# Second linear layer of a graph network: seven products in fourteen batches instead of ten, sums of h made in place, and a new order of VectorE's work

## The chip, the cores and the metric

The kernel runs on one core of one Trainium2 chip. The metric is the device time of one execution in microseconds. Before the change it is 2470.86 us, the median of three runs (2469.76 to 2471.12).

## What is computed

The input x has 16 batches of 1024 rows and 256 channels. A first layer (graph weights, attention with four heads, residual, layer norm) gives x1. The second layer, which the change touches, is

```
agg = A_hat @ x1                        # per batch
h   = relu(batchnorm(agg @ W1.T + b1))  # 512 features, statistics over all batches
o   = h @ W2.T + b2                     # 256 features
out = layernorm(x1 + batchnorm(o))      # statistics of o over all batches
```

All is in float32. Both batch norms need statistics over all 16 batches, so each is a barrier: h is written to HBM as it is made and read back once its statistics are complete, and o is held in SBUF for all batches until its own are complete.

## The kernel before, in words

Matrices are kept transposed, features on the 128 partitions and the 1024 rows of a batch along the free dimension. h of one batch is four blocks of 128 x 1024, one for each 128 of its 512 features. It is loaded as two tiles ("parts"): part i holds blocks i and i + 2. W2 gives two output blocks of 128 x 1024 per batch.

The stage of the second linear layer is the loop over 16 batches at L1798. For each batch ScalarE applies scale, shift and relu of the first batch norm to the four blocks of the next batch's h in place (`scale_shift1`, L1674), PE multiplies, and the result is moved out of PSUM into `o2T[b]` with the bias added; VectorE takes the statistics of four pieces of 128 x 512.

There are two ways to multiply. The undivided one (batches 0 and 11 to 15) uses 16 matmuls of 128 x 512 per batch at L1846 and moves each output block out with one VectorE pass of 128 x 1024 at L1873, followed by two statistics at L1877. The other (batches in `SEVEN`, 1 to 10) treats the product as a 2 x 2 block product and needs seven block products of two matmuls each at L1772: 14 matmuls. It needs four sums of quarters of W2, made once by GpSimd (`left_sums`, into the tile `w2S`), and four sums of quarters of h per batch, made by VectorE (`h_sums`, L1741 to L1752), each on two halves (i = 0 and 1), which is eight instructions of 128 x 512. The sums go into the output tiles of the last four batches, which are not yet in use: batches 12 to 15, two tiles for even and two for odd batches. That is why `SEVEN` ends where it does.

`products` (L637) puts the seven products in the order p1, p6, p2, p7, p5, p4, p3 over three PSUM banks per batch, a, b and c. p1 is copied by ScalarE (L656) into a temporary; p2 is added by PE onto p1 in bank a and moved out by ScalarE (L669). p6 goes into bank b and VectorE adds p1's copy (L648); p7 is added by PE onto p6 in the same bank, which has to wait until VectorE has read it, and VectorE adds p1 again; p4 is added onto that, and VectorE makes an output piece of it. p5 goes into bank c and p3 onto it, each followed by a VectorE add (L679, L687). So VectorE has five passes out of PSUM per batch. The three temporaries lie in the next batch's output tile.

The order of work on PE, ScalarE and VectorE is the order in which the code calls it (`manual_schedule`). [...] The order of the loads on SP is decided by the scheduler. Tiles of h have four buffers, two batches: a load of the next batch's part starts when the batch before the present one has been read for the last time, which is p3's first matmul for part 0 and its second for part 1.

In a seven-product batch b the calls for VectorE were, in order: the third and fourth sums of half 1; a statistic of the batch before; p6's add; two such statistics; p7's add; the statistic (b, 0); p5's add; the first and second sums of the next batch, half 0; p4's add; the same for half 1; p3's add; the third and fourth sums of the next batch, half 0. For batch 1 the sums were made after batch 0's outputs had been moved out and their statistics taken.

After the loop, `coefficients2` gives the second batch norm's scale and shift, and a tail over 16 batches scales o, transposes it on PE, adds x1 (loaded into tiles `xf` by `load_x1`) and applies the layer norm. The x1 of batches 0, 1 and 2 go into three tiles: two held h of batch 0, the third holds `w2S`.

Of the kernel before, what the change touches and what calls it, by code (L numbers as in the profile page):

```python
# [13 lines left out]
ALU = mybir.AluOpType  # L14
# [5 lines left out]
HALF = 512  # L20
# [495 lines left out]
def fast_path(  # L516
# [19 lines left out]
    nc = tc.nc  # L536
    B, N, C = x.shape
# [158 lines left out]

    def right_sums(eng, T, b11, b12, b21, b22):

# [5 lines left out]
    H0, H1 = slice(0, HALF), slice(HALF, N)  # L704
    C0, C1 = slice(0, P), slice(P, C)
# [18 lines left out]
    xp = ctx.enter_context(tc.tile_pool(name="xp", bufs=3))  # L724
# [10 lines left out]
    with (  # L735
# [449 lines left out]
        def run(fs, k):  # L1185
            for f, a in fs[:k]:
                f(*a)
            del fs[:k]
# [135 lines left out]
        with tc.manual_schedule(  # L1324
# [64 lines left out]
            for j in range(len(bursts)):  # L1389
                b, u = j // PERB, j % PERB  # L1390
# [75 lines left out]
            j = len(bursts)  # L1466
# [24 lines left out]
    w1T, w2T = wl["w1T"], wl["w2T"]  # L1491
# [26 lines left out]
    with (  # L1518
# [123 lines left out]
        for b in range(1, B):  # L1642
# [3 lines left out]
            elif b == B - 1:  # L1646
                h0 = []
                for i in range(2):
                    t = xp.tile([P, 2, N], F32, tag="x", name=f"hl_0_{i}")
# [3 lines left out]
            for i, step in enumerate(steps):  # L1653
                step()
                if i == len(steps) - 1 and b < B - 1:
                    later = linear1(b)
# [22 lines left out]
        t = agg.pop(B - 1)  # L1679
# [28 lines left out]
    with tc.tile_pool(name="hl", bufs=4) as hl, tc.tile_pool(name="o2p", bufs=1) as o2p:  # L1708
        o2T = [
            o2p.tile([P, CC, N], F32, tag=f"o2_{b}", name=f"o2_{b}") for b in range(B)  # L1710
        ]
# [3 lines left out]
        def load_x1(b, pool, tag):  # L1715
            xf[b] = pool.tile([P, NCH, C], F32, tag=tag, name=f"xf_{b}")
            nc.sync.dma_start(xf[b], x1_d[b])
# [5 lines left out]
        parts = {}  # L1723

        def load_h(b):
            parts[b] = [hl.tile([P, 2, N], F32, tag="hl", name=f"hl_{b}_{i}") for i in range(2)]
            for i in range(2):
                nc.sync.dma_start(parts[b][i], h_d[b][:, i::2, :])
            hs_of[b] = [parts[b][k % 2][:, k // 2, :] for k in range(HC)]

        SEVEN = range(1, B - 5)
        w2S = xp.tile([P, 4, 2, P], F32, tag="x", name="w2S")
        K0, K1 = slice(0, HC // 2), slice(HC // 2, HC)
        left_sums(
# [1 line left out]
            w2T[:, K0, C0], w2T[:, K1, C0], w2T[:, K0, C1], w2T[:, K1, C1],  # L1738
        )

        def h_sums(b, i, later):  # L1741

            t = parts[b][i]
            T = [o2T[B - 4 + 2 * (b % 2) + j // 2][:, i, (j % 2) * HALF : (j % 2 + 1) * HALF]
                 for j in range(4)]
            b11, b12, b21, b22 = t[:, 0, H0], t[:, 0, H1], t[:, 1, H0], t[:, 1, H1]
            if not later:
                nc.vector.tensor_tensor(T[0], b12, b11, ALU.subtract)
                nc.vector.tensor_tensor(T[1], b22, T[0], ALU.subtract)
            else:  # L1750
                nc.vector.tensor_tensor(T[2], b22, b12, ALU.subtract)
                nc.vector.tensor_tensor(T[3], b21, T[1], ALU.subtract)  # L1752

        def linear2_seven(b):
            X = parts[b]
            hs_of.pop(b)

            def T(j, i):
                return o2T[B - 4 + 2 * (b % 2) + j // 2][:, i, (j % 2) * HALF : (j % 2 + 1) * HALF]

            def mm(k, ps, start):
                for i in range(2):
                    left, right = {
                        1: (w2T[:, i, C0], X[i][:, 0, H0]),
                        2: (w2T[:, 2 + i, C0], X[i][:, 1, H0]),
                        3: (w2S[:, 3, i, :], X[i][:, 1, H1]),
                        4: (w2T[:, 2 + i, C1], T(3, i)),
                        5: (w2S[:, 0, i, :], T(0, i)),
                        6: (w2S[:, 1, i, :], T(1, i)),
                        7: (w2S[:, 2, i, :], T(2, i)),  # L1770
                    }[k]
                    nc.tensor.matmul(  # L1772
                        ps, left, right, start=(start and i == 0), stop=(i == 1),
                        skip_group_check=True,
                    )

            def bank(name):
                if name[0] == "c":
                    return tile_s(name)[:, H0]
                return {"a": tile_o, "b": tile_t}[name[0]](name)  # L1780

            def temps(key, name):
                k = ("p1", "u2", "u3").index(key)
                return o2T[b + 1][:, k // 2, (k % 2) * HALF : (k % 2 + 1) * HALF]

            out = [o2T[b][:, c, hs] for c in range(CC) for hs in (H0, H1)]
            bias = (cols["b2"][:, 0:1], cols["b2"][:, 1:2])
            return products(f"o{b}", bank, out, mm, temps, bias)

        def statistics2(b, i):  # L1790
            c, half = i // 2, i % 2
            nc.vector.bn_stats(
                bn2_st[:, c, 2 * b + half, :], o2T[b][:, c, half * HALF : (half + 1) * HALF]
            )

        load_h(1)
        rest = []
        for b in range(B):  # L1798
            if b + 2 < B and b not in SEVEN:
                load_h(b + 2)  # L1800
            if b in SEVEN:
                nxt = b + 1
                if b > 1:
                    load_h(nxt)
                p1, p6, p2, p7, p5, p4, p3 = linear2_seven(b)
                p1()
                h_sums(b, 1, True)
                run(rest, 1)
                p6()
                run(rest, 1)  # L1810
                p2()
                run(rest, 1)
                for k in (0, 2):
                    scale_shift1(hs_of[nxt][k], k)
                p7()
                statistics2(b, 0)
                p5()
                for k in (1, 3):
                    scale_shift1(hs_of[nxt][k], k)
                if nxt in SEVEN:  # L1820
                    h_sums(nxt, 0, False)
                p4()
                if nxt in SEVEN:
                    h_sums(nxt, 1, False)
                p3()
                if nxt in SEVEN:
                    h_sums(nxt, 0, True)
                rest = [(statistics2, (b, i)) for i in (3, 2, 1)]
                if nxt not in SEVEN:
                    run(rest, 3)  # L1830
                    load_h(nxt + 1)
                continue
            if b + 1 < B:
                for k in (0, 2, 1, 3):
                    scale_shift1(hs_of[b + 1][k], k)
            h = hs_of.pop(b)
            pss = [tile_s(f"po2_{b}_{c}") for c in range(CC if b < B - 1 else CC - 1)]
            last_ps = [tile_o(f"po2_last_{half}") for half in range(2 if b == B - 1 else 0)]

            def half_ps(c, hs):  # L1840
                if last_ps and c == CC - 1:
                    return last_ps[0 if hs == H0 else 1]
                return pss[c][:, hs]

            def mm(c, k, hs):
                nc.tensor.matmul(  # L1846
                    half_ps(c, hs), w2T[:, k, c * P : (c + 1) * P], h[k][:, hs],
                    start=(k == 0), stop=(k == HC - 1),
                )

            if b == 0:

                for ks in (range(HC // 2), range(HC // 2, HC)):
                    for c in range(CC):
                        for k in ks:
                            for hs in (H0, H1):
                                mm(c, k, hs)
            for c in range(CC):
                last = b == B - 1 and c == CC - 1
                if b:  # L1860
                    for k, hs in (
                        [(k, hs) for hs in (H0, H1) for k in range(HC)] if last
                        else [(k, hs) for k in range(HC) for hs in (H0, H1)]
                    ):
                        mm(c, k, hs)
                if last:
                    for hs in (H0, H1):
                        nc.scalar.activation(
                            o2T[b][:, c, hs], half_ps(c, hs), AF.Identity,
                            bias=cols["b2"][:, c : c + 1],  # L1870
                        )
                else:
                    nc.vector.tensor_scalar(  # L1873
                        o2T[b][:, c, :], pss[c], cols["b2"][:, c : c + 1], None, ALU.add
                    )
                for half, hs in enumerate((H0, H1)):
                    nc.vector.bn_stats(bn2_st[:, c, 2 * b + half, :], o2T[b][:, c, hs])  # L1877
                if b == B - 1:
                    coefficients2(c)
            if b == 0:  # L1880
                for i, later in ((0, False), (1, False), (0, True)):
                    h_sums(1, i, later)
            if b >= B - 3:
                load_x1(b - (B - 3), xp, "x")

# [171 lines left out]
```

## Time and profile before

| what | value |
|---|---|
| median of 3 runs | 2470.86 us |
| the profiled execution, time | 2469.28 us |
| its span (first to last instruction) | 2467.5 us |
| PE busy | 2425.2 us, 98% of the span |
| DVE (VectorE) busy | 1840.3 us, 75% |
| ACT (ScalarE) busy | 1231.6 us, 50% |
| POOL (GpSimd) busy | 479.9 us, 19% |
| mean granted TensorE clock | 0.998 |
| stage of the second linear layer, first matmul to the tail's first | 2165.22 to 2373.19 us |
| an f32 matmul of 128 x 512 (L1772) | two records, 592 ns each, started 0.43 us apart |
| a sum of 128 x 512 on VectorE (L1748 to L1752) | 675 to 693 ns |

Times in a trace count from the start of the span. The name a_o stands for bank a of any batch, since buffer numbers are left out, and o for the output tile o2T of any batch, po for the PSUM tile of the undivided way. A line such as L648 is a line of the code above; a line in a helper serves several callers. An arrow <- in square brackets names what ended the idle time before an instruction. PEld is PE's weight load, which carries the waits of the matmul that it precedes. A busy engine isn't a bound by itself: what counts is which engine's work the chain of waits runs through in the stage concerned.

### The profile page before, as it was taken

To read this page: it belongs to the slowest core of one execution; us is meant where nothing else is said; L and a number is where in the kernel's file an instruction comes from. 1 tells how busy PE (TensorE), PEld (TensorE's weight loads), DVE (VectorE), ACT (ScalarE), POOL (GpSimd) and SP (SyncE) were. 2 spreads that over 40 slices of the span, in tenths; PEclk is the share of its full clock that TensorE was granted. 3 is DMA by queue.
4 is the path that set the end of the run, shared out by engine and by line. 5 is a ranking of instruction groups with operands and counts; after the bars stand their busy time and mean duration, and the time that the engine had idled before them with its cause. 6 is when DMAs were issued, how large, how long until landed. Compare 5 with 4: busy or idle time off the path is not lost.

```text
span 2467.5 us, 32796 instructions
## 1 busy us (share of the span) xinstructions
PE 2425.2 (98%) x12462; PEld 1035.2 (42%) x12462; DVE 1840.3 (75%) x2528; ACT 1231.6 (50%) x1535; POOL 479.9 (19%) x487
## 2 busy tenths in 40 slices
PE   8999999999999999999999999999999999999997
PEld 4343443443434434434434343344444444434455
DVE  5678878878888888788788888856555555578568
ACT  6375665765765766757657667311010010144458
POOL 0021112211211211121112113522112212000026
PEclk9999999999999999999999999999999999999999
DMA  3123232332232231323322327222122122255559
GB/s 136 31 48 84 54 53 69 69 51 67 39 82 60 41 86 54 52 69 69 53 68 47 72 52 116 54 101 102 69 86 102 68 85 102 91 200 175 182 190 340
DMA packets 414647, 220.42 MB, mean 89 GB/s; under 512 B 353168, under 2 KB 386448, under 8 KB 406032
## 3 DMA queue, kind: packets, MB, share of 16 engines
q1 hardware_dynamic: 409120, 167.36, 27.6%
q0 software_dynamic: 4832, 50.34, 4.9%
q8 instruction: 100, 1.64, 0.3%
q14 instruction: 67, 0.55, 0.1%
q10 hardware_dynamic: 528, 0.52, 0.1%
HBM read 134.49 MB, written 83.69 MB: 88 GB/s over the span
## 4 chain that ended last, share of the span: by engine, by line
PE 83%; DVE 10%; ACT 3%; DMA 2%; issue 1%; SPq 0%; POOL 0%; DVEq 0%; POOLq 0%
PE ps L1066 17%; PE po L1087 17%; PE pgb L896 7%; PE b_agg L1564 4%; PE pga L896 4%; PE c_agg L1564 4%; PE pk L993 3%; PE po L1846 3%; PE pv L1006 2%; PE a_agg L1564 2%; PE b_h L1596 2%; PE b_o L1772 2%; PE pgc L896 2%; PE pgd L896 2%; PE c_h L1596 2%; PE c_o L1772 1%
## 5 line engine op out<-in xcount | busy, mean ns | idle before, releaser
L1071 ACT ACTIVATE p<-ps 128x1024 f32<-128x1024 f32 x512 | 497.4, 1021 | 182.2 <-PE ps L1066 123.2
L1097 DVE TENSOR_TENSOR acc<-acc,p 128x1024 f32<-128x1024 f32 x384 | 501.4, 1306 | 52.3 <-ACT p L1071 28.9
L1066 PE MATMUL ps<-qT,kT 64*64 64x512 f32 x4096 | 488.3, 592 | 0.3 <-ACT p L1071 0.3
L1087 PE MATMUL po<-p,v 64*64 64x512 f32 x4096 | 485.6, 589 | 0.0
L1161 POOL TENSOR_TENSOR o<-o,r_all 128x512 f32<-128x512 f32 x62 | 95.9, 1555 | 1104.8 <-DVE r_all L1155 989.9
L1087 PEld LDWEIGHTS po<-p,v 64*64 64x64 f32 x4096 | 159.4, 133 | 280.1 <-issue 273.2
L1066 PEld LDWEIGHTS ps<-qT,kT 64*64 64x64 f32 x4096 | 152.4, 133 | 285.9 <-issue 248.5
L847 DVE SCALAR_TENSOR_TENSOR wg<-wg,adj_s 128x1024 f32<-128x1024 f32 x128 | 149.7, 1217 | 24.6 <-ACT wg L843 24.6
L838 ACT ACTIVATE wg<-crow,ccol 128x1024 f32<-128x1024 f32 x128 | 146.7, 1146 | 6.1 <-PE pg L978 6.1
L843 ACT ACTIVATE wg<-wg 128x1024 f32<-128x1024 f32 x128 | 135.9, 1062 | 0.9
L993 PE MATMUL pk<-xT,kvw_s 128*128 128x512 f32 x256 | 121.9, 598 | 3.1 <-ACT drow L1140 3.1
L1006 PE MATMUL pv<-kvw_s,xT 128*128 128x256 f32 x512 | 123.9, 385 | 0.0
L1006 PEld LDWEIGHTS pv<-kvw_s,xT 128*128 128x128 f32 x512 | 95.0, 190 | 50.3 <-issue 13.6
L906 ACT ACTIVATE qT<-qT 128x512 f32<-128x512 f32 x60 | 37.1, 626 | 149.8 <-DVE qT L909 145.3
L896 PE MATMUL pgb<-wg,S 128*128 128x512 f32 x240 | 111.0, 605 | 0.0
L896 PE MATMUL pga<-wg,x 128*128 128x512 f32 x240 | 109.6, 599 | 0.7 <-ACT qT L919 0.7
L1564 PE MATMUL a_agg<-ahT,x1l 128*128 128x512 f32 x240 | 108.1, 593 | 0.7 <-ACT agg L1312 0.7
L1564 PE MATMUL b_agg<-aT,x1S 128*128 128x512 f32 x240 | 107.9, 592 | 0.0
L1162 POOL TENSOR_TENSOR x<-x,o 128x512 f32<-128x512 f32 x62 | 106.9, 1734 | 2.4
L656 ACT COPY p_agg<-a_agg 128x512 f32<-128x512 f32 x15 | 8.8, 586 | 183.3 <-PE a_agg L1564 179.5
L1675 ACT ACTIVATE hl<-hl,bn_sh,bn_sg 128x1024 f32<-128x1024 f32 x64 | 75.6, 1232 | 40.7 <-DMA hl<-h 38.1
L692 POOL TENSOR_TENSOR x1S<-x1l 128x512 f32<-128x512 f32 x15 | 19.4, 1293 | 352.9 <-PE c_agg L1564 350.1
(234 smaller groups left out, 3495.8 us busy)
## 6 DMA issues: line engine op xcount, KB each, us to landing
h<-hw POOLq DMA_DIRECT2D x16, 2048.0 KB, 6.6
hl<-h SPq DMA_DIRECT2D x32, 1024.0 KB
x<-x POOLq DMA_DIRECT2D x16, 1024.0 KB, 4.3
x1l<-x SPq DMA_DIRECT2D x16, 1024.0 KB
xf<-x SPq DMA_DIRECT2D x16, 1024.0 KB
o<-oS SPq DMA_DIRECT2D x62, 256.0 KB
o<-o SPq DMA_DIRECT2D x248, 64.0 KB
x<-in_x_dram SPq DMA_DIRECT2D x15, 1024.0 KB
```

The costliest lines, as they stand in the source:

```text
L838: nc.scalar.activation(w, s["crow"], AF.Abs, bias=s["ccol"][:, n : n + 1])
L843: nc.scalar.activation(w, w, AF.Tanh, scale=0.5)
L847: nc.vector.scalar_tensor_tensor(w, w, 1.0, adj_s[:, n, :], op0=ALU.subtract, op1=ALU.mult)
L896: nc.tensor.matmul(ps, left, right, start=(start and i == 0), stop=(i == NCH // 2 - 1), skip_group_check=True,)
L993: nc.tensor.matmul(ps, kvw_s[:, c, kc * P : (kc + 1) * P], s["xT"][:, c, hs], start=(c == 0), stop=(c == CC - 1),)
L1006: nc.tensor.matmul(pt[:, j * C : (j + 1) * C], s["xT"][:, c, n * P : (n + 1) * P], kvw_s[:, c, C : 2 * C], start=(c == 0), stop=(c == CC - 1),
L1066: nc.tensor.matmul(ps[kh * D : (kh + 1) * D, hd * HALF : (hd + 1) * HALF], kT[r, pr, ks], qT[r, pr, qh * HALF : (qh + 1) * HALF], start=Tr ...
L1071: nc.scalar.activation(p, ps, AF.Exp)
L1087: nc.tensor.matmul(g["po"][kh][hd * D : (hd + 1) * D, :], s["v"][r, m, h * D : (h + 1) * D], p[r, hd * HALF : (hd + 1) * HALF], start=(m = ...
L1097: nc.vector.tensor_add(g["acc"], g["acc"], p)
L1162: nc.gpsimd.tensor_tensor(xs, xs, o, ALU.add)
L1564: nc.tensor.matmul(ps, left, right, start=(start and i == 0), stop=(i == NCH // 2 - 1), skip_group_check=True,)
```

## The change

`SEVEN` grows from batches 1 to 10 to batches 1 to 14. The sums of h no longer need four spare output tiles: three of the four overwrite a quarter of h that no later product needs, and one goes into a quarter of the last batch's output tile (`second_sum`; even and odd batches have a half each). Since a sum overwrites h, the third sum now waits until p1 has read its quarter, and the fourth until p2 has. The temporaries of `products` go into the batch's own output pieces. The calls are reordered, so that VectorE has mostly one statistic or one sum between two of its passes out of PSUM, where there were up to four. The first two sums of batch 1 are called ahead of batch 0's moves out of PSUM. The calls of `load_x1` for batches 0 and 1 stay at batches 13 and 14, the one for batch 2 comes after the loop.

```
-        SEVEN = range(1, B - 5)
+        SEVEN = range(1, B - 1)
...
+        def second_sum(b, i):
+            return o2T[B - 1][:, b % 2, i * HALF : (i + 1) * HALF]
+
+        def h_sums(b, k, ks=range(2)):
+
+            for i in ks:
+                t, T2 = parts[b][i], second_sum(b, i)
+                dst, one, two = {
+                    1: (t[:, 0, H1], t[:, 0, H1], t[:, 0, H0]),
+                    2: (T2, t[:, 1, H1], t[:, 0, H1]),
+                    3: (t[:, 0, H0], T2, t[:, 0, H0]),
+                    4: (t[:, 1, H0], t[:, 1, H0], T2),
+                }[k]
+                nc.vector.tensor_tensor(dst, one, two, ALU.subtract)
...
-                        4: (w2T[:, 2 + i, C1], T(3, i)),
-                        5: (w2S[:, 0, i, :], T(0, i)),
-                        6: (w2S[:, 1, i, :], T(1, i)),
-                        7: (w2S[:, 2, i, :], T(2, i)),
+                        4: (w2T[:, 2 + i, C1], X[i][:, 1, H0]),
+                        5: (w2S[:, 0, i, :], X[i][:, 0, H1]),
+                        6: (w2S[:, 1, i, :], second_sum(b, i)),
+                        7: (w2S[:, 2, i, :], X[i][:, 0, H0]),
...
             def temps(key, name):
-                k = ("p1", "u2", "u3").index(key)
-                return o2T[b + 1][:, k // 2, (k % 2) * HALF : (k % 2 + 1) * HALF]
+                return out[{"p1": 2, "u2": 1, "u3": 3}[key]]
...
                 p1()
-                h_sums(b, 1, True)
+                run(rest, 1)
+                h_sums(b, 3)
                 run(rest, 1)
                 p6()
                 run(rest, 1)
                 p2()
+                h_sums(b, 4)
                 run(rest, 1)
                 for k in (0, 2):
                     scale_shift1(hs_of[nxt][k], k)
                 p7()
-                statistics2(b, 0)
-                p5()
                 for k in (1, 3):
                     scale_shift1(hs_of[nxt][k], k)
-                if nxt in SEVEN:
-                    h_sums(nxt, 0, False)
+                ahead = [(h_sums, (nxt, k, (i,))) for i in range(2) for k in (1, 2)]
+                if nxt not in SEVEN:
+                    ahead = []
+                run(ahead, 1)
+                p5()
+                run(ahead, 1)
                 p4()
-                if nxt in SEVEN:
-                    h_sums(nxt, 1, False)
+                run(ahead, 2)
                 p3()
-                if nxt in SEVEN:
-                    h_sums(nxt, 0, True)
-                rest = [(statistics2, (b, i)) for i in (3, 2, 1)]
+                rest = [(statistics2, (b, i)) for i in (3, 2, 0, 1)]
                 if nxt not in SEVEN:
-                    run(rest, 3)
-                    load_h(nxt + 1)
+                    run(rest, 4)
+                if b >= B - 3:
+                    load_x1(b - (B - 3), xp, "x")
                 continue
...
             if b == 0:
+                for k in (1, 2):
+                    h_sums(1, k)
...
-            if b == 0:
-                for i, later in ((0, False), (1, False), (0, True)):
-                    h_sums(1, i, later)
-            if b >= B - 3:
-                load_x1(b - (B - 3), xp, "x")
+        load_x1(2, xp, "x")
```

More of the change, by code (lines that the diff above doesn't have):

```diff
@@ L1739, in fast_path @@
         )
[L1741 to L1752, printed above, removed]
+        def second_sum(b, i):
[10 more added lines that the diff above has]
+                nc.vector.tensor_tensor(dst, one, two, ALU.subtract)
         def linear2_seven(b):
@@ L1756, in linear2_seven @@
             hs_of.pop(b)
-            def T(j, i):
-                return o2T[B - 4 + 2 * (b % 2) + j // 2][:, i, (j % 2) * HALF : (j % 2 + 1) * HALF]
             def mm(k, ps, start):
```

## The prediction

> **What bounds the kernel now.** I read the page's first two parts first: PE is busy 98% of the span and its clock is granted in full in all 40 slices, so time is gained only where PE waits or where PE is given fewer matmuls. Next the chain of work that ended last, in order of time (columns: start us, length us, what), for the stage that the diff touches. Its beginning and end:
>
> ```profile
> 2165.22 14.02 PE po L1846 x32
> ...
> 2179.26 1.29 DVE o L1873
> ...
> 2181.87 0.60 DVE o L1748
> ...
> 2187.06 0.67 DVE o L648
> ...
> 2187.78 1.98 PE b_o L1772 x4
> ```
>
> The chain leaves PE at 2179.26 and comes back at 2187.78: VectorE moves batch 0 out of PSUM, takes its statistics and only then makes the sums that batch 1's products need. Later the chain is PE alone up to the tail:
>
> ```profile
> 2304.69 61.80 PE po L1846 x144
> 2366.49 6.88 PE po_last L1846 x16
> 2373.39 0.70 ACT o L1868
> ```
>
> Then the busy time of each engine in stretches, cut at the first matmul of batches 1, 2, 10, 11, 12 and 15:
>
> ```profile
> 2179.06:2194.74 15.68, 12.78 (x29) 5.07 (x28) 12.69 (x19) 5.79 (x6) 0.00 (x0) 1.00 0.20 68
> 2194.74:2206.94 12.20, 12.20 (x29) 5.24 (x28) 10.74 (x18) 6.02 (x6) 0.00 (x0) 1.00 0.56 173
> ...
> 2304.52:2318.25 13.73, 13.73 (x33) 6.08 (x32) 5.05 (x7) 4.74 (x4) 0.00 (x0) 1.00 0.69 232
> ```
>
> The columns are length, PE, PEld, DVE, ACT, POOL, clock, DMA share, GB/s. Batch 1 takes 15.68 us, batches 2 to 10 take (2304.52-2194.74)/9 = 12.20, batches 11 to 15 take (2373.19-2304.52)/5 = 13.73. A product is two 128x512 matmuls (four records) and the chain gives it 1.72 us (12.02 for seven; eight would be 13.73, which is the undivided batch). So a seven-product batch has 0.18 us of waiting in it. Where, the waits in 2194.74 to 2304.52 say (columns: total us, times, longest), and VectorE's timeline in batch 2:
>
> ```profile
> PEld b_o L1772 <- DVE o L648: 6.7, 9, 0.8
> ```
>
> ```profile
> 2198.58 0.68 DVE L1792 BATCH_NORM_STATS2 bn_st<-o 128x6 f32<-128x512 f32 x1
> 2199.18 0.73 DVE L648 SCALAR_TENSOR_TENSOR o<-b_o,col_b,o 128x512 f32<-128x512 f32 x1
> ...
> 2204.31 0.68 DVE L1748 TENSOR_TENSOR o<-hl 128x512 f32<-128x512 f32 x1
> 2205.10 0.69 DVE L1749 TENSOR_TENSOR o<-hl,o 128x512 f32<-128x512 f32 x1
> 2205.71 0.74 DVE L648 SCALAR_TENSOR_TENSOR o<-b_o,col_b,o 128x512 f32<-128x512 f32 x1
> ```
>
> Product 6 ended at 2198.2, but VectorE was in four sums and a statistic and added it from 2199.18 to 2199.91; product 7, due at 2199.90 into the same bank, started at 2199.97 and ran 0.1 longer. Two further lines: when the next batch's h is there (ScalarE's timeline), and what held VectorE before batch 0 (its own timeline).
>
> ```profile
> 2201.20 2.37 ACT L1675 ACTIVATE hl<-hl,bn_sh,bn_sg 128x1024 f32<-128x1024 f32 x2 [0.36 <-DMA hl<-h]
> 2203.73 2.37 ACT L1675 ACTIVATE hl<-hl,bn_sh,bn_sg 128x1024 f32<-128x1024 f32 x2 [0.16 <-DMA hl<-h]
> ```
>
> ```profile
> 2175.96 1.28 DVE L1873 TENSOR_SCALAR o<-po,col_b 128x1024 f32<-128x1024 f32 x1 [9.01 <-DMA h<-hw]
> ```
>
> [...] here independent operations of 0.68 start 0.60 apart (2196.17, 2196.77, 2197.37), and a dependent one 0.79 apart (2204.31, 2205.10). The trace decides: 0.60, and 0.18 more for a dependence. [...]
>
> **The change part by part.** Times are from a batch's first matmul. PE: p1 0, p6 1.72, p2 3.43, p7 5.15, p5 6.87, p4 8.58, p3 10.30, next batch 12.02. VectorE starts 0.22 after a product's end (2201.99 for a product that ended at 2201.79).
>
> (1) Batches 11 to 14 become seven-product: 4 x (13.73-12.02) = **6.84 us** off PE, which is the path there.
>
> (2) Start of batch 1. Its first two sums now stand ahead of batch 0's move out of PSUM. ScalarE has batch 1's h ready at 2174.5 (2168.77 + 5.76 for five activations). The first sum into the last batch's output tile now carries the wait for the h<-hw write that L1873 had, over at 2175.9; that write is issued before anything that changed. Behind it in VectorE's queue: two sums to 2177.15, the two moves and four statistics to 2182.2 (the move now begins 1.2 late, and had 0.7 of waiting before its second half), step 3 of the sums to 2183.4, p6's add to 2184.15. Product 7 is due at 2179.06 + 5.15 = 2184.21. It just fits, and a stall here is at most the 0.2 that such a miss cost before. p6 has its sum at 2177.2, due 2180.78. So 15.68 becomes 12.02: **3.66 us**.
>
> (3) The new order in batches 2 to 10. I walk VectorE's queue with 0.60 per sum, statistic or plain add and 0.66 per fused add (2199.18 to 2199.83): p4's add of the batch before at -1.50, two dependent sums to 0.54, p3's add to 1.14, a statistic to 1.74, step 3 (waits for p1, each half, 1.08 and 1.94) to 2.94, a statistic to 3.54, p6's add at 3.65, ready at 4.40; a statistic to 4.91, step 4 (waits for p2, 4.5 and 5.4) to 6.11, a statistic to 6.71, p7's add at 7.09, ready 7.84; a sum to 8.35, p5's add at 8.80, ready 9.49; a sum to 10.0; p4's add at 10.52 = -1.50 + 12.02. It closes. Work: 8 sums and 4 statistics and 2 adds at 0.60, 3 at 0.66, 0.18 for one dependence: 10.56 of 12.02. Spare ahead of PE: p7 5.15-4.40 = 0.75, p4 8.58-7.84 = 0.74, p3 10.30-9.49 = 0.81, p6 1.72-0.6 = 1.1. Before, p4 and p3 had 0.77 and 0.82 and lost nothing. So 9 x 0.18 = **1.6 us**; next late is PE itself.
>
> In-place sums: the trace has no such subtraction. Nearest is acc<-acc,p, in place, 1306 ns for 1024 columns against 1286 for a plain 1024 pass. I take 0.60; with no overlap at all (0.69) eight cost 0.7 more, inside the 1.46 spare. [...]
>
> (4) Waits added. Sums of step 1 and 2 for the next batch wait for ScalarE, which waits for h's load, and now stand ahead of p5's, p4's and p3's adds, so p3 and the next p7 wait behind them. Loads are there at 6.46 and 8.99 (2201.20, 2203.73 less 2194.74), an activation takes 1.23: rows ready 7.7, 8.9, 10.2, 11.4; the sums want them at 7.75, 9.40, 11.18 and about 11.9. Nothing waits. p3 keeps its time until the first load is 1.1 later, the next p7 until the second is 1.3 later. Batch 10 had 6.29 and 8.82.
>
> (5) Moved loads. On SP only one place changes: x1 of batch 2 stood after batch 10 (issued 2305.33) and now stands behind h of batch 15 and x1 of batch 3, waiting for the left sums' tile at batch 14's end. That packs 3 MB into batch 15's 13.7 us with no h load beside it; h's 2 MB take 9 us (2194.13 to 2203.7), so 3 MB about 13.5. Residual 2 reads it at 2388.71, 29 us after. POOL's queue is the same. Cost nothing.
>
> (6) Temporaries in the batch's own output tile and statistics' order: the same instructions, nothing. Batch 15 and the tail keep their form.
>
> Sum: 6.84 + 3.66 + 1.6 = 12.1. Span 2467.5 becomes 2455.4; with the 1.78 around it (2469.28 - 2467.5) 2457.2. The median is 1.58 above the profiled execution, so **2458.8**.
>
> **Rivals.** (A) As above, within a microsecond: 0.70. (B) VectorE's queue leaves a stall such as today's 0.18 to 0.25 in each of 14 batches: 2.5 to 3.5 less, about 2461.8. For it: 88% busy and each spare is below 0.85. Against: p4 and p3 run with the same spare today. 0.13. (C) The tail gives part back, waiting for x1 loads: 2462 to 2471, say 2465. Against: 15 us to spare. 0.06. (D) The change doesn't do what it says at the start: the h<-hw write holds the sums and with them the moves of batch 0, and batch 1 still takes 15.7: 2462.5. Only if that write lands over 3 us later. 0.03. (E) h's loads move onto the path a little, half a microsecond in 13 batches: 2465.3. 0.04. (F) **Slower**: h's load sets the batch. In VectorE's queue the next batch's sums hold back p5's add, hence p3. Each microsecond that the load is later than today's plus 1.1 costs a microsecond in 13 batches; it decides from 12.1/13 = 0.93 over, that is from a first load at 8.5 instead of 6.46. At 9.5 the time is 2458.8 + 13 x 1.9 = 2484. Against: the same two transfers, released at the same point (after p3's first half), with 173 GB/s in the batch. 0.04.
>
> **From these to the numbers.** About 0.2% (4.9 us, 2465.9) is what a measurement of this kernel tells from no change. Faster by more: A, B, D, most of C and E: 0.91. Within: 0.05. Slower: F, 0.04. The range 2456.5 to 2464 holds A, B, D and part of C, 0.87; the bounds of in-place sums and of product 7's first stall lie inside. Its low end is A with the medians' own scatter and a microsecond of tail.
>
> **What would show it.** In the new trace: batches 1 to 14 at 12.02 to 12.05 each, the next batch's p1 directly after p3; no wait of PEld b_o for L648 beyond the first batch; the add at L648 0.22 after its product; chain from 2165.22 to the tail on PE alone; batch 15 ends near 2361.1 instead of 2373.19. Wrong: a DVE sum at 7.8 us that waits for ACT or DMA (E, F), p7 that starts after 5.2 (B), a first residual that waits for xf (C).

## The result, and the profile after

The changed kernel takes 2456.36 us, the median of six runs (2455.62 to 2458.24), against 2470.70 (2469.76 to 2471.75) for six runs of the kernel before. The ratio is 0.9942 (95% interval 0.9932 to 0.9952): faster by 14.3 us. The prediction was 2458.8 with a range from 2456.5 to 2464.0. The sign and the mechanism came as forecast; the time lies 0.14 us below the range. The profiled execution of the kernel after takes 2458.24 us, the slowest of its six, with a span of 2456.5.

First the chain of waits of the kernel after over the same stage (start us, length us, what). Before, it left PE for VectorE from 2179.26 to 2187.78; now it stays on PE from batch 0 to the last batch:

```profile
2165.49 14.00 PE po L1846 x32
2179.49 1.72 PE a_o L1771 x4
2181.21 1.72 PE b_o L1771 x4
...
2347.72 6.87 PE po L1846 x16
2354.59 6.88 PE po_last L1846 x16
2361.47 0.02 issue
2361.50 0.70 ACT o L1870
```

From 2179.49 to 2347.72 are 168.24 us, 14 batches of 12.017. The same in the table of stretches of the kernel after, cut at batch 1, batches 2 to 10, 11 to 14, and 15 (length, then busy time of PE, PEld, DVE, ACT, POOL, then clock, DMA share, GB/s):

```profile
2179.30:2191.32 12.02, 12.02 (x29) 5.32 (x28) 9.88 (x16) 5.79 (x6) 0.00 (x0) 1.00 0.24 87
2191.32:2299.48 108.16, 108.16 (x253) 47.88 (x252) 97.46 (x154) 54.09 (x54) 0.00 (x0) 1.00 0.55 175
2299.48:2347.55 48.07, 48.07 (x113) 21.28 (x112) 41.54 (x65) 23.95 (x24) 0.00 (x0) 1.00 0.56 175
2347.55:2361.30 13.75, 13.75 (x34) 6.08 (x33) 7.89 (x14) 0.69 (x1) 0.55 (x1) 1.00 0.59 229
```

PE is busy for the whole of every stretch. From the first product of batch 1 to the first matmul of the tail the stage took 194.13 us before (2179.06 to 2373.19) and takes 181.97 now (2179.33 to 2361.30). The difference, 12.16, is the prediction's 12.1. VectorE's timeline in batch 2 of the kernel after (by the table it began at 2191.32; start, length, operation, in brackets the idle time before it):

```profile
2195.05 0.75 DVE L648 SCALAR_TENSOR_TENSOR o<-b_o,col_b,o 128x512 f32<-128x512 f32 x1
2195.72 0.68 DVE L1790 BATCH_NORM_STATS2 bn_st<-o 128x6 f32<-128x512 f32 x1
2196.32 1.27 DVE L1754 TENSOR_TENSOR hl<-hl,o 128x512 f32<-128x512 f32 x2
2197.51 0.68 DVE L1790 BATCH_NORM_STATS2 bn_st<-o 128x6 f32<-128x512 f32 x1
2198.42 0.75 DVE L648 SCALAR_TENSOR_TENSOR o<-b_o,col_b,o 128x512 f32<-128x512 f32 x1 [0.22 <-PE b_o L1771]
2199.08 0.68 DVE L1754 TENSOR_TENSOR hl<-hl 128x512 f32<-128x512 f32 x1
2200.13 0.69 DVE L679 TENSOR_TENSOR o<-c_o,o 128x512 f32<-128x512 f32 x1 [0.36 <-PE c_o L1771]
```

The adds out of PSUM stand 3.73, 7.10 and 8.81 after the batch's start; the walk had 3.65, 7.09 and 8.80. At the second and third VectorE now waits for PE (0.22, 0.36). At the first, p6's add, for which product 7 waited before, it waits for nothing, and the sum is ready at 4.48, where product 7 starts at 5.18 (2196.50 less 2191.32). Two sums in place, which the trace of before could not show, take 1.27 for both: less the 0.68 of one, the second starts 0.59 after the first, where 0.60 was taken. At the start of batch 1:

```profile
2175.63 1.29 DVE L1754 TENSOR_TENSOR o<-hl 128x512 f32<-128x512 f32 x2 [1.24 <-DMA h<-hw]
2176.84 1.28 DVE L1875 TENSOR_SCALAR o<-po,col_b 128x1024 f32<-128x1024 f32 x1
...
2182.05 1.27 DVE L1754 TENSOR_TENSOR hl<-o,hl 128x512 f32<-128x512 f32 x2
2183.25 0.74 DVE L648 SCALAR_TENSOR_TENSOR o<-b_o,col_b,o 128x512 f32<-128x512 f32 x1
```

The wait for the h<-hw write went over to the sums, as forecast, and p6's add begins at 2183.25 (forecast 2183.4). Product 7 did not have to wait.

So the stage is as predicted, and the miss lies in how the sum was carried to the medians: 14.3 was measured, 12.1 was reckoned. What the experiments had to settle was whether the change gives 12.1 us and the rest comes from which executions were compared, or whether it gives more than its own trace shows, and by what.

### The profile page after: what moved, and what is told of

Same layout as the page of the kernel before. It is cut to its first block, busy times and chain, and to the rows that moved or that the text cites. A ratio compares the mean times of both kernels' runs of the same rounds, so it can differ in the third digit from the quotient of the medians.

```text
span 2456.5 us, 32863 instructions
## 1 busy us (share of the span) xinstructions
PE 2418.9 (98%) x12446; PEld 1033.7 (42%) x12446; DVE 1863.6 (76%) x2572; ACT 1236.0 (50%) x1543; POOL 478.5 (19%) x487
## 4 chain that ended last, share of the span: by engine, by line
PE 84%; DVE 10%; ACT 3%; DMA 2%; issue 1%; SPq 0%; POOL 0%; POOLq 0%; DVEq 0%
PE ps L1066 17%; PE po L1087 17%; PE pgb L896 7%; PE b_agg L1564 4%; PE pga L896 4%; PE c_agg L1564 4%; PE pk L993 4%; PE b_o L1771 3%; PE pv L1006 2%; PE a_agg L1564 2%; PE b_h L1596 2%; PE pgc L896 2%; PE pgd L896 2%; PE c_o L1771 2%; PE a_o L1771 2%; PE c_h L1596 2%
## 5 line engine op out<-in xcount | busy, mean ns | idle before, releaser
L1095 DVE TENSOR_TENSOR acc<-p,p 128x1024 f32<-128x1024 f32 x64 | 77.3, 1208 | 7.5 <-ACT p L1071 7.5
```

## The experiments

Twelve runs in three groups; within a group they share the runs of the kernel before. "After" below is the changed kernel.

**again: the kernel after, unchanged**

> The changed kernel once more, with five rounds and a second profile. Theory 1 (the change is worth 12.1 us and the rest of the measured 14.3 us is run-to-run drift of other stages): the stretch from batch 1's first matmul to the tail's first is 181.98 us again, within 0.05; the median ratio moves towards 0.9951 and the span changes by what the clock does at the tail's start (0.86 granted in the first profile, 1.1 us). Theory 2 (the change also gains about 2 us somewhere that the first profile didn't show): the ratio stays at 0.994 and some stage outside that stretch is shorter than before by 1 to 2 us in this profile.

Measured: 2460.09 us (2458.02 to 2461.31) against 2471.72 (2469.35 to 2474.34), ratio 0.9951 (0.9937 to 0.9964): 11.6 us less, not 14.3. The 14 batches take 168.24 again. The stage began 2.4 us later than in the first profile (2167.87 against 2165.49), though nothing had been changed; a part of the reason is found below. The two sets of runs of the same two kernels differ by 2.7 us in what they call the saving, so one set alone doesn't settle a microsecond.

**ten: seven products in batches 1 to 10 only, with the new order**

```
-        SEVEN = range(1, B - 1)
+        SEVEN = range(1, B - 5)
...
                     run(rest, 4)
+                    load_h(nxt + 1)
...
+            if B - 3 <= b < B - 1:
+                load_x1(b - (B - 3), xp, "x")
```

> Seven products in batches 1 to 10 only, with the sums in place and the new order (batches 11 to 14 undivided, as before). Theory 1: loses 4 x 1.71 = 6.84 us against the changed kernel, so 2463.2 us beside a changed kernel of 2456.4; each undivided batch 13.73, each divided one 12.02. Rival (the order of VectorE's work is worth more than the batches): it stays within 3 us of the changed kernel.

Measured: 2465.30 us, ratio 0.9972 (0.9960 to 0.9983). In the trace ten batches take 120.17 us, 12.017 each, and the five undivided ones 68.68; to the tail that is 6.86 more than after. By medians in the same group it is 5.2 more (2465.30 against 2460.09), with the start of the stage differing between executions as told above. Term (1) of the prediction, 6.84, is right; terms (2) and (3) hold without it.

**late_first: the first two sums of batch 1 go back behind batch 0's moves and statistics**

```
             if b == 0:
-                for k in (1, 2):
-                    h_sums(1, k)
                 for ks in
...
+            if b == 0:
+                for k in (1, 2):
+                    h_sums(1, k)
```

> The changed kernel, but the first two sums of batch 1 stand behind batch 0's moves and statistics on VectorE. Theory 1: product 6 of batch 1, due at 1.72 us after the batch's first matmul, waits for four sums that end some 5 us after it; batch 1 takes 14.6 to 15.0 instead of 12.02, 2.6 to 3.0 us lost. Rival (batch 0's moves out of PSUM are the true wait): no more than 0.5 us lost.

Measured: 2462.18 us, ratio 0.9964 (0.9951 to 0.9978). Batch 1 takes 16.77 us in place of 12.02, which is 4.75 more; the expectation was 2.6 to 3.0. Its chain:

```profile
2179.64 1.72 PE a_o L1771 x4
2181.36 2.82 issue
2184.18 2.38 PE b_o L1771 x4
2186.57 2.98 PE a_o L1771 x4
2189.55 1.72 PE b_o L1771 x4
```

The wait is 2.82, as reckoned. The profile names no releaser for it ("issue"), but VectorE makes the two sums that this product reads at just that time, and PE starts when the first of them is done:

```profile
2183.39 1.29 DVE L1754 TENSOR_TENSOR o<-hl 128x512 f32<-128x512 f32 x2
```

But the two products after it take 2.38 and 2.98 where a product takes 1.72: another 1.92. The stretches of the same kernel show why; the clock is the third number from the end:

```profile
2184.00:2186.00 2.00, 1.82 (x4) 0.97 (x5) 1.88 (x4) 0.00 (x0) 0.00 (x0) 0.89 0.04 12
2186.00:2188.00 2.00, 2.00 (x3) 0.67 (x2) 0.75 (x1) 0.00 (x0) 0.00 (x0) 0.50 0.00 0
2188.00:2190.00 2.00, 2.00 (x5) 0.94 (x4) 1.11 (x2) 0.41 (x1) 0.00 (x0) 0.75 0.00 0
```

After the wait the granted clock is 0.5 for a while. The missing shares, (0.11 + 0.50 + 0.25) x 2 us, come to 1.72 us of full clock, which is 3.4 us at half clock. This gave a third theory: a gap in PE's work such as this one of 2.82 us costs more than its length, because the clock can be halved after it. The kernel before has a gap of 2.42 us in batch 1 (idle ahead of its second product), and the change removes it. In the profile that the prediction read, the clock there was 1.00. By medians of its group this kernel is only 2.1 us above the kernel after (2460.09); what else differs between executions is found below.

**bulk: the three statistics of the batch before together ahead of p6's add**

```
-                run(rest, 1)
+                run(rest, 3)
                 p6()
-                run(rest, 1)
                 p2()
                 h_sums(b, 4)
-                run(rest, 1)
```

> The changed kernel, but three of the four statistics of the batch before stand together ahead of product 6's add, instead of one in each gap. Theory 1 (place in the queue matters, not VectorE's spare time): product 6's add starts at 4.74 instead of 3.65 us of its batch and product 7, due at 5.15, starts at 5.5 to 5.6 in 13 batches, 5 to 7 us lost. Rival (10.56 us of work in 12.02 leaves room for any order): nothing lost.

Measured: 2464.76 us, ratio 0.9972 (0.9961 to 0.9984). The same instructions in another order, with two statistics moved to stand ahead of p6's add beside the one that was there: 14 batches take 174.38 us, 6.14 more, 0.44 each (5 to 7 in all were expected; by medians of the group it is 4.7). The last of three lines is p6's add, in VectorE's timeline of this kernel, and below it PE's, where p6 ended at about 2206.8:

```profile
2204.95 1.27 DVE L1754 TENSOR_TENSOR hl<-o,hl 128x512 f32<-128x512 f32 x2
2206.14 1.87 DVE L1790 BATCH_NORM_STATS2 bn_st<-o 128x6 f32<-128x512 f32 x3
2207.93 0.73 DVE L648 SCALAR_TENSOR_TENSOR o<-b_o,col_b,o 128x512 f32<-128x512 f32 x1
```

```profile
2206.63 1.88 PE L1771 MATMUL a_o<-hl,w12T 128*128 128x512 f32 x4
2208.71 1.98 PE L1771 MATMUL b_o<-hl,w2S 128*128 128x512 f32 x4 [0.20 <-DVE o L648]
```

The add comes at 2207.93, over a microsecond after its product, and product 7 waits for it (due 2208.35, after p2's 1.72). So the order is what term (3) lives on: with VectorE at about nine tenths (97.46 us of 108.16 in batches 2 to 10 of the kernel after), two statistics in the wrong gap are a stall in every batch.

**before_again_1 and before_again_2: the kernel before, two more profiles**

> The kernel before, profiled again. Theory 1 (the change's worth is 12.1 us and no more): batch 1 takes 15.68 us again at full clock. Theory 3 (formed after the run of late_first, where a gap of 2.8 us on PE in batch 1 brought half the clock for some 3.4 us and cost 1.7 us more): in a part of the executions of the kernel before, its own gap of 2.4 us in batch 1 does the same; batch 1 then takes about 17.3 us, and the change is worth 1.7 us more in those than the first profile let see.

> The kernel before, a third profile, for the same question: batch 1 at 15.68 us (theory 1), or 17.3 us with a granted clock below 1 in the 4 us after the gap (theory 3).

Measured: 2474.08 and 2470.49 us. Batch 1 takes 16.88 and 16.59 us, against 15.68 in the profile that was shown first: 1.2 and 0.9 more, with the same gap of 2.41 and 2.42. The expected 17.3 was too much, since part of the stretch at half clock falls on a second wait. First the chain of before_again_1, then its stretches:

```profile
2187.26 1.96 PE b_o L1772 x2
2189.22 2.58 PE a_o L1772 x4
2191.80 1.72 PE b_o L1772 x4
```

```profile
2186.00:2188.00 2.00, 1.75 (x3) 0.57 (x4) 1.90 (x4) 0.00 (x0) 0.00 (x0) 0.85 0.04 12
2188.00:2190.00 2.00, 2.00 (x4) 0.80 (x3) 2.00 (x4) 0.00 (x0) 0.00 (x0) 0.50 0.00 0
2190.00:2192.00 2.00, 2.00 (x5) 0.83 (x4) 0.28 (x1) 0.16 (x1) 0.00 (x0) 0.79 0.00 0
```

Again (0.15 + 0.50 + 0.21) x 2 / 0.5 = 3.4 us at half clock. The third theory holds in two profiles of three, with a price of about one microsecond.

**warm: the kernel after, with three more matmuls in PE's gap at the start of the tail**

```
-            add_x1(0, 2)
-            add_x1(0, 3)
+            for pair in (2, 3, 2, 3, 2):
+                add_x1(0, pair)
```

Each of these writes x1 into the same place anew, so they are only work for PE.

> The changed kernel with three more matmuls (2.6 us) at the tail's start, in the 3.2 us in which PE waits for the second batch norm's coefficients; they repeat two that stand there, so nothing else changes. Theory 3: the clock stays at 1.00 at the tail's start in every execution, the tail's first residual comes 1.1 us earlier than in the two profiles of the changed kernel, and the median falls by 0.5 to 1.1 us. Rival (the clock isn't what costs the 1.1 us): no difference, or slower.

Measured: 2456.91 us (2455.94 to 2459.82), ratio 0.9945 (0.9931 to 0.9958). The gap ahead of the transposes, in which PE waits for the second batch norm's coefficients, in PE's timeline of the kernel after and then of this one:

```profile
2366.26 1.66 PE L1925 MATMUL pf<-ident,o 128*128 128x128 f32 x7 [2.98 <-ACT o L1901]
2367.71 2.96 PE L1942 MATMUL held<-ident,o 128*128 128x128 f32 x16
```

```profile
2365.57 0.98 PE L1925 MATMUL pf<-ident,o 128*128 128x128 f32 x7 [0.41 <-ACT o L1901]
2366.39 1.95 PE L1942 MATMUL held<-ident,o 128*128 128x128 f32 x16
```

With the gap filled the sixteen matmuls take 1.95 us instead of 2.96. But in one of the three profiles of the kernel after they take 1.95 without any filler (again_2, below), so this one profile does not show that the filler did it. In the times a gain over the kernel after can't be told: that kernel had 2456.36, 2457.26 and 2460.09 in its three sets.

**stats_twice: every statistic of a seven-product batch is taken twice**

```
-            nc.vector.bn_stats(
+            for _ in range(2):
+                nc.vector.bn_stats(
```

> The changed kernel with every statistic of the seven-product batches taken twice (same result): 2.4 us more for VectorE per batch, 12.96 of 12.02. Theory 1 (VectorE has 1.46 us to spare and no more): walked through the queue, a batch takes 13.24 instead of 12.02 and 13 batches lose 12 to 16 us. Rival (VectorE is far from a bound): no more than 5 us.

Measured: 2484.23 us, ratio 1.0046 (1.0031 to 1.0062). 14 batches take 192.01 us, 23.8 more than after; 12 to 16 were expected. VectorE is now busy almost without a gap and sets the batch, at 13.83 us from 2234.67 to 2248.50. The expectation had each repeat at 0.60. VectorE's timeline has two of them in 1.41, so the second starts 0.73 after the first. The third line below is its only wait in the batch:

```profile
2235.82 1.41 DVE L1791 BATCH_NORM_STATS2 bn_st<-o 128x6 f32<-128x512 f32 x2
2237.15 1.27 DVE L1754 TENSOR_TENSOR hl<-o,hl 128x512 f32<-128x512 f32 x2
2246.99 0.75 DVE L648 SCALAR_TENSOR_TENSOR o<-b_o,col_b,o 128x512 f32<-128x512 f32 x1 [0.28 <-PE b_o L1771]
```

Four repeats of 0.73 are 2.92 in a batch with 12.02 - 10.56 = 1.46 spare by the prediction's walk. That leaves 1.46 over; 13.83 - 12.02 = 1.81 was measured. The other 0.35 is that wait: the sum before it starts at 2246.03, so p4's add comes 0.96 after it in place of 0.60. The 10.56 of the walk is confirmed: 13.83 - 0.36 - 2.92 = 10.55. The expectation failed on the repeat's price and on this wait.

**before_warm: the kernel before, with one idle product in the gap of batch 1**

```
                 p1()
+                if b == 1:
+                    spare = tile_o("spare")
+                    for i in range(2):
+                        nc.tensor.matmul(
+                            spare, w2T[:, i, C0], parts[b][i][:, 0, H0], start=(i == 0), stop=(i == 1)
+                        )
```

Two matmuls go to a bank that nothing reads.

> The kernel before with two more matmuls (1.7 us, into a bank that nobody reads) behind product 1 of batch 1, in the 2.4 us in which PE waits for the sums; the result is the same. Theory 3: batch 1 takes 15.68 us at a clock of 1.00, as in the first profile alone of three, and the median falls by 0.7 to 1.2 us against the kernel before. Theory 1: batch 1 and the median as in the kernel before.

Measured: 2470.02 us (13 runs, 2469.00 to 2472.95) against 2471.62 (17 runs, 2469.99 to 2474.25), ratio 0.9994 (0.9986 to 1.0003). The filled gap is 0.70 us, and batch 1 takes 15.69 at a clock of 1.00. By medians the filler is worth 1.6 us, but the interval reaches just past no change, so the times alone don't prove it. One profile at full clock doesn't either, since one of three had it without the filler. The mean granted clock of every execution says more: it is 0.997 or above in 12 of these 13 executions and in 2 of the 17 of the kernel before, which have 0.996 otherwise. What such a step means is told below.

**again_2: the kernel after, in the same group**

> The changed kernel a third time, on the same chip as the kernel before with its gap filled. Theory 3: some 13 to 13.5 us under the kernel before (12.1, and 1.0 for the clock in batch 1), and 12.1 under the one with the filled gap; its stretch of seven-product batches is 168.24 us again.

Measured: 2457.26 us (2456.16 to 2457.99), ratio 0.9943 (0.9929 to 0.9956). It is 14.4 us below the kernel before (13 to 13.5 were expected) and 12.8 below the one with the filled gap (12.1 were expected). Its profile has no half clock at the start of the tail (the sixteen matmuls take 1.95 us), and a span of 2454.4.

**load_late: from batch 3 on, a small load ahead makes the first part of h land late**

```
+            if 2 < b < B - 1:
+                nc.sync.dma_start(parts[b][0][:, 0, 0:256], h_d[b][:, 0, 0:256])
             for i in range(2):
                 nc.sync.dma_start(parts[b][i], h_d[b][:, i::2, :])
```

> The changed kernel, but from batch 3 on part 0 of h waits for a small load into the same tile, so that it comes second; its rows are then there some 2.5 us later than today (9 to 10 us after a batch's start instead of 6.5). The slower rival of the prediction: behind the late sums stand p5's add and with it p3; 1.4 to 2 us lost in each of 12 batches, 17 to 24 us in all. If the sums' place in VectorE's queue does no harm: under 5 us.

Measured: 2485.63 us, ratio 1.0063 (1.0047 to 1.0078): slower than before. The 14 batches take 28.0 us more than after; 17 to 24 were expected. ScalarE's, VectorE's and PE's timelines of batch 2, which began at 2190.90:

```profile
2200.64 4.63 ACT L1675 ACTIVATE hl<-hl,bn_sh,bn_sg 128x1024 f32<-128x1024 f32 x4 [3.70 <-DMA hl<-h]
```

```profile
2201.91 0.69 DVE L1756 TENSOR_TENSOR hl<-hl 128x512 f32<-128x512 f32 x1 [3.19 <-ACT hl L1675]
2202.52 0.69 DVE L679 TENSOR_TENSOR o<-c_o,o 128x512 f32<-128x512 f32 x1
```

```profile
2203.26 1.98 PE L1773 MATMUL c_o<-hl,w2S 128*128 128x512 f32 x4 [1.90 <-DVE o L679]
```

The load is there at 9.74 after the batch's start, where the kernel after has it at 6.46 (2197.78 less 2191.32, the value of before). VectorE's sum waits 3.19 for it, p5's add stands behind the sum, and p3 waits 1.90 for the add. Rival F gave the price in advance: a microsecond for each that the load comes later than 6.46 + 1.1. That is 9.74 - 7.56 = 2.18; the batch took 14.18, which is 2.16 more. Two batches are longer, the next one (15.34) and one more (15.41), and there the mean clock is 0.79 from 2216 to 2224 and from 2248 to 2256, as much as 3.4 us at half clock would make of 8 us. Of the next one:

```profile
2217.62 3.01 PE L1773 MATMUL c_o<-hl,w2S 128*128 128x512 f32 x4 [2.08 <-DVE o L679]
```

So the clock fell there after a gap of 2.08 us, shorter than the 2.42 of batch 1. The kernel after has a margin of 1.1 us before this begins (9.74 - 6.46 - 2.16).

**one_twice: one statistic per batch is taken twice**

```
-            nc.vector.bn_stats(
+            for _ in range(2 if i == 0 else 1):
+                nc.vector.bn_stats(
```

> The changed kernel with one statistic of each seven-product batch taken twice, the one behind product 6's add (0.73 us more for VectorE per batch, 11.3 of 12.02; same result). Theory 1: it falls into the gap ahead of product 7's add, which starts at 7.4 instead of 7.09 us and is ready 0.4 us ahead of product 4; nothing lost, within 1 us. Rival (any added work is paid): 9.5 us lost in 13 batches.

Measured: 2458.24 us (2456.67 to 2460.84), ratio 0.9947 (0.9932 to 0.9962). The stage stays at 168.2. The repeat stands in the gap ahead of p7's add, whose result is ready 8.23 after the start of batch 3 (2210.02 + 0.73 less 2202.52) and is needed at 8.58. With bulk and stats_twice this says that VectorE can take one more instruction of 0.7 us per batch there, that four more are too many, and so are two of its own statistics moved ahead of p6's add.

## Why the prediction was right, and where it missed

**(1) Batches 11 to 14, 6.84:** right. The trace has 4 x 1.71, and ten gives it back (6.86).

**(2) Batch 1, 3.66:** the mechanism is right and the size too small. From the profile that was read, 15.68 becomes 12.02, exactly. But that profile was the one of three without half clock after the gap of batch 1, and the clocks of 39 further executions, below, say that it was a rare one. The other two give 16.88 and 16.59, so what the change removes is 3.7, 4.6 or 4.9. The prediction took the clock of 1.00 in one execution's row for a property of the kernel. The page's row of 40 slices, which it read as a clock granted in full, can't tell: a slice is 61.7 us long, and 1.7 us lost in it leaves 0.97, which is printed as 9 too. The row is 9 throughout for before_again_1 as well.

**(3) The new order, 9 x 0.18 = 1.6:** right; the nine batches take 108.16 in place of 109.78. That the order does it, and not the sums in place, bulk shows: it keeps these, and takes 12.46 a batch (174.38 / 14). One sign came out otherwise than forecast, which had no wait of PEld b_o for L648 after the first batch. In 2179.3 to 2361.3 there is one in each batch (total us, times, longest):

```profile
PEld b_o L1771 <- DVE o L648: 3.4, 14, 0.2
```

It costs nothing here: it is the weight load that waits, and PE's own busy time fills every stretch.

**(4) The added waits, nothing:** right: the first load is at 6.46, the 7.56 allowed isn't reached. Rival F's mechanism is real, at the price given, but wasn't met.

**(5) and (6), moved loads and temporaries, nothing:** right. The tail's first 11.80 us have PE busy for 8.82 us in both kernels, before and then after, and in neither tail does an engine wait for a load of x1:

```profile
2373.20:2385.00 11.80, 8.82 (x56) 6.58 (x55) 8.36 (x26) 10.93 (x12) 1.49 (x2) 1.00 0.47 178
```

```profile
2361.30:2373.10 11.80, 8.82 (x47) 7.07 (x46) 7.39 (x23) 10.93 (x12) 0.55 (x1) 0.86 0.47 178
```

The clock of 0.86 in the second is the half clock after the tail's own gap (0.50 from 2367 to 2369), which costs about a microsecond: from the tail's first matmul to the end of the span are 95.2 us here and 94.2 in again_2, which has the full clock. Both kernels have that gap, so it comes and goes in both.

**From the span to the median, + 1.58: the step that failed.** "The median is 1.58 above the profiled execution" was taken over as a fixed offset. It was not one: the measured median lies 0.84 below the 2457.2 that was worked out for the profiled execution (2457.2 - 2456.36), and these 2.4 us are the whole miss. The profiled execution of before was free of half clock in batch 1, at the tail and at the end of attention (a third gap, below); that of after was the slowest of its six. What separates executions can be read off the spans, from 2467.5 for before and the predicted 2455.4 for after, both for a stage that begins at 2165.22:

| profile | span | stage begins, against 2165.22 | half clock in batch 1, at the tail | worked out |
|---|---|---|---|---|
| before, the first | 2467.5 | 0 | none, none | 2467.5 |
| before_again_1 | 2472.3 | + 2.6 | 1.2, 1.1 | 2472.4 |
| before_again_2 | 2468.6 | - 0.6 | 0.9, 1.1 | 2468.9 |
| after, the first | 2456.5 | + 0.3 | none, 1.1 | 2456.8 |
| again | 2459.0 | + 2.6 | none, 1.1 | 2459.1 |
| again_2 | 2454.4 | - 0.8 | none, none | 2454.6 |
| warm | 2454.8 | - 0.4 | none, none | 2455.0 |

Each agrees to 0.3 us. Of each of the two late starts, 2.6, some 1.6 us are half clock too, at attention's end around 1542 us: the clock of the two stretches 1540 to 1544 and 1544 to 1548 is 0.85 and 0.72 in again, 0.79 and 0.79 in before_again_1, and 1.00 in before. In again the first matmul after the gap there starts 1.07 later than in before (1542.41 against 1541.34), and the po product soon after it 2.72 later (1546.81 against 1544.09). The 1.07 that came ahead of the half clock is not explained.

For the executions without a trace there is one figure, the mean granted clock. Every profile has the half clock in its last microseconds (0.50 from 2445 to 2456 in the first profile of the kernel after), after PE's last matmul (which ends at 2442.2 there), where it costs PE nothing. Beyond that, the mean is 0.998 in the three of the fourteen profiles that have no stretch of 3.4 us at half clock, 0.997 in those with one, and 0.996 in those with two or three; one_twice has 0.997 with one stretch of some 5.7 us (below). So the figure is a rough count of stretches. Executions by that clock:

| kernel, set | 0.998 | 0.997 | 0.996 |
|---|---|---|---|
| before, 39 in the three groups | 1 | 4 | 34 |
| before_warm, 13 | 1 | 11 | 1 |
| after, the first six | 3 | 3 | 0 |
| again, 5 | 0 | 1 | 4 |
| again_2, 5 | 1 | 4 | 0 |
| warm, 5 | 3 | 2 | 0 |

The profile from which the prediction was made had 0.998, as 1 of these 39 has, so it was not a typical execution of the kernel before. With batch 1's gap filled, most executions have one stretch fewer. And the spans of the 16 executions of the kernel after fall apart by clock, whatever their set: 2453.8 to 2454.4 at 0.998, 2455.2 to 2456.5 at 0.997, 2457.9 to 2459.5 at 0.996. So the sets that gave 14.3 and 11.6 differ in the main by how many stretches their executions had. Both again and again_2 ran on the same chip; why the one has more is open. Nor is the clock everything: the execution of before at 0.998 has a span of 2469.0, 1.5 longer than the first profile.

Of the 1.58, about 1.05 (the mean of 1.2 and 0.9) was the half clock after batch 1's gap, which the change takes away, and so should not have been carried over. That makes the gain 12.1 + 1.05 = 13.2 by medians, where two of the three measured differences are 14.3 and 14.4 and the third is 11.6; their mean is 13.4. Against before_warm, without that effect, 12.8 is left. The single differences scatter by more than what remains open, a microsecond or so. In the first set the tail is a likely place for it: by their clock half of these executions have no stretch at all, so none at the tail either, where both further profiles of before have one. That is inferred from the clocks and not shown by traces. The low end of the range, "A with the medians' own scatter and a microsecond of tail", knew none of this, and was 0.14 too high.

## What to carry to other kernels

Before a saving is carried from one profile to a median, take a second profile of the same kernel, and compare the mean clock of the profiled execution with that of the others: here the same gap cost 2.4 us of waiting alone in one execution and about a microsecond more in two others, and 0.998 against 0.996 would have told it. The change, in closing that gap, gained the gap and, in most executions, the half clock after it. And walk VectorE's queue instruction by instruction, in the order of the calls: in bulk an add whose product was ready came over a microsecond late, at 2207.93, behind the three statistics called before it. The same instructions, two statistics moved ahead of one add, took back 6.1 of the 12.1 us, and a load 3.3 us late took back all of them and more.

## What the runs showed of the hardware

**Half clock after short gaps.** After some gaps in PE's work the granted clock was 0.50. By the missing shares it was so for 3.4 us in late_first, in before_again_1 and twice in load_late (0.79 over 8 us). At the tail it is worked out from PE's timeline: from the first matmul after the gap to the next held<-xf matmul PE took 3.48 us in again_2, 5.12 in the first profile of the kernel after and 6.33 in one_twice. These are 1.64 and 2.85 us more, so an estimated 3.3 and 5.7 us at half clock. The gaps with half clock after them: 2.08 and 2.59 us in load_late, 2.41 and 2.42 in batch 1 (two profiles of three; the third has 2.42 too, at a clock of 1.00), 2.82 in late_first, 2.64 (again) and 2.95 (before_again_1) at attention's end, and 2.97 or 2.98 at the tail's start (9 of 13 profiles without the filler). The other ten waits of load_late, up to 1.97, left the clock alone, and so did gaps of 1.54 (the first profile of the kernel after) and 2.69 (the first of the kernel before) at attention's end. So the length alone doesn't decide: 2.08 was enough in one place, and 2.98 was not in four profiles. What else does, no run shows.

**A repeated statistic** into the same six columns starts 0.73 us after the first (1.41 for two in stats_twice), statistics into different columns 0.60 (1.87 for three in bulk).
